# A four-layer graph network on one core: degree products of 128 columns, three products of ones ahead of one block's degrees, and row-sum copies moved ahead of the first gathered group

## The chip, the cores and the metric

The kernel runs on one core of a Trainium2 chip. The metric is the device time in microseconds (us); before the change three executions took 830.39, 831.70 and 832.74 us, median 831.7. A fourth execution was taken by the profiler; the profile and the prediction's sums are of that one. In the texts, PE is TensorE (matrix products; PEld is its weight load), ACT is ScalarE, DVE is VectorE, POOL is GpSimd and SP is the engine whose queue issues most transfers. "L964" is line 964 of the kernel before.

## The reference, cut to what matters

Four graph layers follow each other on `x` (2708 nodes, 128 features) with the same dense 2708 x 2708 matrix `adj`, each with a residual and a layer norm. The change touches the first two.

```python
# layer 0
A_hat  = A + eye;  degree = A_hat.sum(axis=1)
d      = degree ** -0.5                     # 0 where infinite
h      = (d[:, None] * A_hat * d[None, :]) @ X
x      = layernorm(x + h @ W.T + b)
# layer 1
XW     = x @ W
Z1     = leaky_relu((XW @ a_row)[:, None] + (XW @ a_col)[None, :], 0.01)
den    = exp(Z1);  num = A @ den            # num is summed over all nodes
att    = where(num != 0, den / num, 0)
x      = layernorm(x + A @ (att @ XW))
```

Layers 2 and 3 are further products with `A` (a hyperbolic layer, and one with the signs of `A`), and the kernel's change does not touch their code.

## The kernel before, in words

**Stage one, the first 120 us or so.** The transpose of `adj` is read in tiles of 512 x 512, `A{d}_{c}`: row block `d` and column block `c`, six blocks each way, the last only 148 wide. A loop over `c` (the lines up to L1280) loads the six tiles of one column block, lets ACT check them for negative values (`check`, L1236), lets DVE add them into one tile `part` (L1261, L1263), and then calls `degrees(c, part)` (L953). That folds `part` twice on DVE (L957, L958) and sums it over its 128 partitions on PE: for each of the four tiles of 128 nodes, the product of a 128 x 128 piece of `part`, as weights, with one column of ones (L964). In the traces one product of float32 operands is recorded as two matrix instructions, so a block's degrees are eight instructions. ACT then takes the square root (L975), DVE inverts it and scales the block's rows of `z = x @ W0.T`, which live in the tile `q_b` (L976 to L979), and copies the raw degrees to `row_sum` (L981).

The products with the adjacency itself are `multiply(d, c, ...)` (L940): four products of 128 x 512 into the accumulator of block `c`, with the scaled rows of block `d`. A tile above the diagonal (`d < c`) is multiplied when it is read; those on and below it are kept, and come when the degrees of their own rows are known: `row_products(c)` does row block `c` up to the diagonal. In the loop, block 1 calls `row_products(0)` ahead of its degrees, then sixteen products of bfloat16 ones (`keep_busy`, L265, into an accumulator not begun yet), and its degree products are put behind these. Blocks 2, 3 and 4 call `row_products(c - 1)` after their own degrees. `prepare_finish` (L787), called in block 2's turn, adds a few products of one or two columns (L789, L795, L800, L807).

**What sets the order.** Each engine runs its queue in the order in which it was written out. The programming framework writes it: it takes an instruction by its place in the program, but puts a later one ahead where it expects the earlier one not to be ready yet. `tc.issue_after(i)` puts the instructions of its block behind `i` on `i`'s engine, and `queued(engines)` chains all that is so marked in program order. From the trace, PE did 16 instructions of L940 between the degrees of blocks 0 and 1, then the ones, then 34 (two ahead of block 1's degrees, 32 behind) up to block 2's degrees. By their number these 34 are `multiply(0, 2)`, `multiply(1, 2)`, the whole of `row_products(1)` (16) and one product of block 3.

**Up to 225 us** the second half of layer 0 and the preparation of layer 1 follow: norms, the keys of nodes, sorting nodes into groups (24 groups of about 126, `GM`), and one-row sums over all nodes (`whole_sum`, L878), whose products fill PE between other work. These sums end in two PSUM banks, `tot[0]` and `tot[1]`: columns 0 to 2047 in four rows of the first, the rest in five pieces of the second. `sums_out` (L1479) copies pieces of them with ACT (L1482) into row 0 of `carry0`. It is called twice: for the first three pieces, columns 0 to 1535, during the sort, and for the other six at the second place described below.

**The grouped attention, from 225 us.** `adj` is split in two halves of 1354 columns. For each half and each group `q`: POOL gathers the 128 rows of the group (L1606) into one of four places; `carry` (L1637) puts the sums of `carry0` on rows 0 and 1 of the first group of a half; `numerators(q)` runs three products (L1655) into three PSUM tiles. For each of the three, DVE copies two rows to the next group's place (L1658, later L1673), and ACT takes the logarithm (L1660). Behind the third product's logarithm, ACT makes a later group's matrix (L760) from a product on PE (L757). `weighted(q - 1)` has DVE form an exponent (L1686) and ACT its exponential (L1722), and `aggregate(q - 2)` multiplies (L1750). The second `sums_out` stands in this loop at `q == 0`, behind `numerators(0)`; the second half's `carry`, at group 24, is its only reader. In the first three groups the PSUM tiles rotate over five places, so that the third product of group 2 takes the place of the first of group 1.

Of the kernel before, what the change touches and what calls it, by code (L numbers as in the profile page):

```python
# [15 lines left out]
AF = mybir.ActivationFunctionType  # L16
# [5 lines left out]
P = 128  # L22
# [3 lines left out]
NB = (N + BW - 1) // BW  # L26
# [50 lines left out]
def rows(t):  # L77
    return min(P, N - t * P)


def width(b):
    return min(BW, N - b * BW)


def tiles(b):
    return range(b * (BW // P), min(NT, (b + 1) * (BW // P)))
# [3 lines left out]
def kernel(  # L90
# [20 lines left out]
    nc = tc.nc  # L111
# [8 lines left out]
    ones = const.tile([P, P], F32, tag="ones", name="ones")  # L120
# [8 lines left out]
    one_c = const.tile([P, 1], F32, tag="one", name="one_c")  # L129
# [43 lines left out]
    row_sum = const.tile([P, NT], F32, tag="row_sum", name="row_sum")  # L173
# [40 lines left out]
    def acc_tile(b, name):  # L214
        return psum.tile([P, BW], F32, tag=f"acc{b}", name=name)

    def ps_tile(name):
        return psum.tile([P, BW], F32, tag="ps", name=name, bufs=2)
# [43 lines left out]
    def keep_busy(dst, n):  # L262

        for _ in range(n):
            last = nc.tensor.matmul(  # L265
                dst, lhsT=ones_b, rhs=ones_b.unsqueeze(1).to_broadcast([P, 4, P]), start=True, stop=True
            )
        return last.ins
# [110 lines left out]
    def c_tile(name, n=NT):  # L379
        return col.tile([P, n], F32, tag=name, name=name)  # L380
# [483 lines left out]
    sums_of = [(c, 0, BW, 32 * c, 0, 0) for c in range(4)]  # L864
# [50 lines left out]
    with tc.tile_pool(name="tri", bufs=1) as tp:  # L915
# [4 lines left out]
        acc = [acc_tile(b, f"a0_{b}") for b in range(NB)]  # L920
# [30 lines left out]
        busy = {}  # L951

        def degrees(c, part):  # L953

            w, ts = width(c), tiles(c)
            n = len(ts)
            nc.vector.tensor_add(part[:, :2, :w], part[:, :2, :w], part[:, 2:, :w])  # L957
            nc.vector.tensor_add(part[:, 0, :w], part[:, 0, :w], part[:, 1, :w])  # L958
            pd = ps_tile(f"deg{c}")
            full = [t for t in ts if rows(t) == P]  # L960
            for i, t in enumerate(ts):
                kw = rows(t)
                with tc.issue_after(busy[c]) if c in busy else nullcontext():
                    nc.tensor.matmul(  # L964
                        pd[:kw, i : i + 1], lhsT=part[:, 0, i * P : i * P + kw], rhs=ones[:, 0:1], start=True, stop=True
                    )

            span = slice(ts[0], ts[-1] + 1)
            dc = dcol[:, span]
            root = c_tile(f"droot{c}", n)  # L970
            if len(full) < n:
                nc.gpsimd.memset(root, 1.0)
            ends = [(P, 0, len(full))] + [(rows(ts[-1]), n - 1, n)] * (len(full) < n)
            for kw, ia, ib in ends:
                rooted = nc.scalar.activation(root[:kw, ia:ib], pd[:kw, ia:ib], AF.Sqrt, bias=one_c[:kw, :])  # L975
            nc.vector.scalar_tensor_tensor(dc, root, 0.0, root, op0=ALU.is_equal, op1=ALU.add)  # L976
            nc.vector.reciprocal(dc, dc)
            nc.vector.scalar_tensor_tensor(dc, root, 0.0, dc, op0=ALU.not_equal, op1=ALU.mult)
            scaled = nc.vector.tensor_mul(z[:, span, :], z[:, span, :], dc.unsqueeze(2).to_broadcast([P, n, F]))  # L979
            for kw, ia, ib in ends:  # L980
                nc.vector.tensor_copy(row_sum[:kw, ts[0] + ia : ts[0] + ib], pd[:kw, ia:ib])  # L981
            return scaled.ins, [rooted.ins]

        def unit(c):
# [238 lines left out]
        def sum_rows(n):  # L1223
            with queued(PE):
                whole_sum(n)
# [18 lines left out]
        rooted = []  # L1244
        centred(range(NB))
        for c in range(NB):
            w = width(c)
            part = ut[:, : 4 * BW].rearrange("p (t c) -> p t c", c=BW)
            at = {}
            for d in range(NB):  # L1250
                at[d] = load_tile(d, c)
                nt = len(tiles(d))
                if d < NB - 2:
                    check(d, c, at[d])
                    if (d, c) == (1, 0):
                        with tc.issue_after(checks[d, c]):
                            load_later()
                if d == 1:

                    with tc.issue_after(scaled) if scaled is not None else nullcontext():  # L1260
                        nc.vector.tensor_add(part[:, :, :w], at[0][:, :, :w], at[1][:, :, :w])  # L1261
                elif d > 1:
                    nc.vector.tensor_add(part[:, :nt, :w], part[:, :nt, :w], at[d][:, :nt, :w])  # L1263
                if d < c:
                    multiply(d, c, at[d])
                if d >= min(c, NB - 2):
                    kept[d, c] = at[d]
            if c == 1:
                product = row_products(c - 1)
                with tc.issue_after(product):  # L1270
                    busy[c] = keep_busy(acc[NB - 1], 16)
            scaled, rooted[:] = degrees(c, part)
            for d in range(NB - 2, NB):
                check(d, c, at[d])
            if c < NB - 2:
                unit(c)
            if 1 < c < NB - 1:
                row_products(c - 1)
            if c == 2:
                prepare_finish()  # L1280
# [52 lines left out]
    with ctx_keep:  # L1333
# [11 lines left out]
        with tc.tile_pool(name="sort", bufs=1) as st_p:  # L1345
# [11 lines left out]
            with queued(PE):  # L1357
                nc.tensor.matmul(
                    lim_v, lhsT=upper, rhs=filled_b[:, :, 1:], start=True, stop=False, skip_group_check=True
                )  # L1360
                for q in range(1, BQ):
                    nc.tensor.matmul(
                        lim_v[:, :, q],
                        lhsT=ones_b,
                        rhs=filled_b[:, :, before[q - 1]],
                        start=False,
                        stop=(q == BQ - 1),
# [87 lines left out]
            for i in range(2):  # L1455
                for h, (ta, tb) in enumerate(((0, t_a), (t_a, NT))):
                    low[i, h] = acc_tile(2 + 2 * i + h, f"low{i}_{ta}")
                    nn = (tb - ta) * GM
                    with queued(PE):
                        nc.tensor.matmul(  # L1460
                            low[i, h][:, :nn],
                            lhsT=upper,
                            rhs=oh[i][:, ta:tb, :],
                            start=True,
                            stop=False,
                            skip_group_check=True,
                        )
                        for t in range(tb - 1):
# [3 lines left out]
                                lhsT=ones_b,  # L1472
                                rhs=oh[i][:, t, :].unsqueeze(1).to_broadcast([P, tb - first, GM]),
                                start=False,
                                stop=(t == tb - 2),
# [3 lines left out]
            def sums_out(parts):  # L1479
                for c, a, b, o, bank, at in parts:  # L1480
                    with queued(ACT):
                        nc.scalar.copy(carry0[0:1, c * BW + a : c * BW + b], tot[bank][o : o + 1, at : at + b - a])  # L1482
# [3 lines left out]
            for i in range(2):  # L1486
# [12 lines left out]
                for t in range(NT):  # L1499
                    ohs = srt([P, P], f"ohs{i}_{t}", BF16, 10, "ohs")  # L1500
                    nc.vector.tensor_scalar(ohs, iota_b, slot[:, i, t : t + 1], None, op0=ALU.is_equal)
                    with queued(PE):
                        nc.tensor.matmul(
                            ps[:, : 6 * GM],
                            lhsT=ohs,
                            rhs=val[i][:, t, :, :].rearrange("p n g -> p (n g)"),
                            start=(t == 0),
                            stop=(t == NT - 1),
# [46 lines left out]
            with queued(ACT):  # L1555
                for g in range(FIRST):
                    group_matrix(w_first, g, gb[:, g, :])
            sum_rows(2)

    marks = {}  # L1560

# [27 lines left out]
    def grouped_attention(u_sb, rows_g):  # L1589
        adj_h = adjT.rearrange("k (h w) -> (k h) w", h=2)  # L1590
        chunks = [(0, BW), (BW, 2 * BW), (2 * BW, HALF)]
        with (
# [198 lines left out]
            for q in range(2 * GM + 2):  # L1791
                if q + 3 < 2 * GM:
                    behind = gather(q + 3)
                    if q == 3:
                        marks["begun"] = behind
                        with queued(ACT):
                            nc.scalar.dma_start(out=x_d, in_=x)
                    if q + 3 < GM:
                        group_xw(q + 3, behind)
                t = q - GM - 3  # L1800
                if 0 <= t < HALF // P:
                    with queued(PE, ACT):
                        node_major_u(t, True)
                if q == GM + GM // 4:
                    with tc.issue_after(behind):
                        fit_nodes()
                if q == GM:
                    with queued(DVE):
                        repeated(x, NF * P)
                if q == GM + 2:  # L1810
                    with queued(PE, DVE, ACT):
                        tail_factors()
                if q == GM + GM // 2:
                    with queued(DVE):
                        added_up()
                if q == GM + GM // 2 + 4:
                    with queued(PE, DVE):
                        checked()
                if q == 2 * GM - 4:
                    marks["flag"] = nc.values_load(flag_i, min_val=0, max_val=1)  # L1820
                if q < 2 * GM:
                    numerators(q)
                if q == 0:
                    sums_out(sums_of[3:])
                if 0 < q <= 2 * GM:
                    weighted(q - 1)
                if q > 1:
                    aggregate(q - 2)
# [894 lines left out]
```

## Time and profile before

| | |
|---|---|
| three executions | 830.39, 831.70, 832.74 us |
| profiled execution, its own time | 832.59 us |
| its span, first to last instruction | 830.8 us (1.8 us lie outside) |
| mean granted PE clock over the span | 0.990 |
| busy: PE, DVE, ACT, POOL | 796.2, 620.4, 518.6, 139.1 us |
| PE idle from 234.5 us on, longest piece | 0.8 us |
| degree products (L964), all blocks | 44 instructions |
| copies of the row sums (L1482) | 9, from 213.9 to 231.2 us |

A profile is one execution, taken by the hardware profiler. The table of busy time tells how much each engine worked, the chain of waits tells which piece of work was last to arrive at each point, followed back from the end, and the timeline lists the instructions of an engine in order of time with the idle time before them and who ended it. A table by stretches gives, for each stretch of the span, the busy time of each engine (with a count of instructions), the share of the full PE clock that was granted, the busy share of the DMA engines and GB/s. Times in these views count from the start of the span.

### The profile page before, as it was taken

How to read it: one execution, taken by the hardware profiler on the slowest of the kernel's cores; microseconds unless marked ns; L12 is line 12 of the kernel's file. 1: busy time of each engine (PE TensorE's matmuls, PEld its weight loads, DVE VectorE, ACT ScalarE, POOL GpSimd, SP SyncE). 2: the span in 40 equal slices, each digit the busy share in tenths (PEclk: the TensorE clock that was granted, in tenths of full speed). 3: DMA queues.
4: the chain of work that ended last, by engine and by line, in shares of the span. 5: the costliest groups of instructions: out<-in, count | busy, mean ns of one | idle time of the engine just before them, and what ended most of it. 6: DMA issues, size and time to landing. Idle time of an engine off the chain costs nothing.

```text
span 830.8 us, 10374 instructions
## 1 busy us (share of the span) xinstructions
PE 796.2 (96%) x3418; PEld 449.8 (54%) x3418; DVE 620.4 (75%) x1458; ACT 518.6 (62%) x929; POOL 139.1 (17%) x173
## 2 busy tenths in 40 slices
PE   4699999999999999999999999999999999999996
PEld 4244454454345555455554455564455666677774
DVE  3786645579689999789996677997588863776674
ACT  4955554314298998788886333696455665666662
POOL 5232000001386663162201000000000000000000
PEclk9899999999999999999999999999999999999999
DMA  9998659079589555436435778795984751856600
GB/s 341 358 384 288 142 52 358 27 262 382 174 300 391 193 164 156 142 96 213 152 101 180 269 270 296 237 336 201 358 287 156 239 190 56 291 190 243 219 36 16
DMA packets 94986, 181.71 MB, mean 219 GB/s; under 512 B 6272, under 2 KB 37396, under 8 KB 94584
## 3 DMA queue, kind: packets, MB, share of 16 engines
q1 hardware_dynamic: 85228, 142.62, 50.4%
q0 software_dynamic: 7680, 34.85, 12.9%
q10 hardware_dynamic: 2016, 3.49, 1.2%
q8 instruction: 29, 0.48, 0.2%
q14 instruction: 33, 0.27, 0.1%
HBM read 176.68 MB, written 4.28 MB: 218 GB/s over the span
## 4 chain that ended last, share of the span: by engine, by line
PE 82%; DVE 9%; DMA 5%; ACT 2%; issue 1%; SPq 1%; DVEq 0%; ACTq 0%
PE a L2052 17%; PE num L1655 13%; PE uacc L1750 11%; PE a L940 9%; PE a L2565 7%; PE a L2549 6%; PE a_u L1920 5%; DMA A<-in_adjT_dram 4%; PE a L1920 2%; PE t L878 2%; DVE jk L1413 2%; PE upper L1740 1%; PE pp L2452 1%; DVE ut L1263 1%; SPq L898 1%
## 5 line engine op out<-in xcount | busy, mean ns | idle before, releaser
L1660 ACT ACTIVATE ln<-num,inval,occ_l 128x512 f32<-128x512 f32 x144 | 99.2, 725 | 24.5 <-PE num L1655 18.2
L940 PE MATMUL a<-A,q_b 128*128 128x512 f32 (+2 forms) x264 | 109.5, 564 | 3.3 <-DVE q_b L979 3.3
L1655 PE MATMUL num<-rows_g,w_all 128*128 128x512 f32 (+1 forms) x252 | 104.5, 542 | 0.0
L1750 PE MATMUL uacc<-att,xw_g 128*128 128x512 f32 (+1 forms) x248 | 99.7, 534 | 1.4 <-issue 1.3
L2549 PE MATMUL a<-mask,node 128*128 128x452 f32 (+1 forms) x252 | 94.7, 458 | 0.0
L2052 PE MATMUL a<-cb,q_b 128*128 128x512 f32 (+1 forms) x222 | 89.5, 540 | 0.0
L1673 DVE COPY rows_g<-num 2x512 f32<-2x512 f32 x129 | 75.1, 611 | 15.6 <-ACT ln L1660 12.7
L2532 ACT ACTIVATE mask<-cb 128x904 fp32r<-128x904 f32 (+2 forms) x66 | 60.8, 922 | 34.6 <-PE a L2549 31.7
L2052 PE MATMUL a<-cb,xw 128*128 128x512 f32 (+1 forms) x196 | 79.6, 532 | 0.0
L1686 DVE SCALAR_TENSOR_TENSOR att<-q_b,e_l,ln 128x1354 f32<-128x1354 f32 (+2 forms) x50 | 77.8, 1559 | 2.1 <-ACT ln L1660 2.1
L940 PEld LDWEIGHTS a<-A,q_b 128*128 128x128 f32 (+1 forms) x264 | 46.6, 194 | 51.4 <-issue 47.3
L1606 POOL DMA_INDIRECT rows_g<-in_adjT_dram,row_i x48 | 54.1, 1127 | 116.3 <-PE num L1655 83.6
L1655 PEld LDWEIGHTS num<-rows_g,w_all 128*128 128x128 f32 x252 | 45.5, 190 | 48.9 <-issue 38.3
L2565 PE MATMUL a<-cb,edge 128*128 128x452 f32 (+1 forms) x150 | 68.9, 543 | 0.0
L1722 ACT ACTIVATE att<-att,e_l 128x1354 f32<-128x1354 f32 (+2 forms) x50 | 68.6, 1377 | 0.4 <-DVE att L1686 0.4
L1750 PEld LDWEIGHTS uacc<-att,xw_g 128*128 128x128 f32 x248 | 46.9, 190 | 38.6 <-issue 24.8
L2549 PEld LDWEIGHTS a<-mask,node 128*128 128x128 f32 x252 | 46.2, 189 | 26.6 <-issue 24.1
L1236 ACT ACTIVATE xw<-A 128x2048 f32<-128x2048 f32 (+3 forms) x36 | 57.0, 1582 | 2.7 <-DMA A<-in_adjT_dram 1.8
L2052 PEld LDWEIGHTS a<-cb,q_b 128*128 128x128 f32 x222 | 38.4, 190 | 31.6 <-issue 29.4
L1906 ACT ACTIVATE a_s<-cb 128x512 fp32r<-128x512 f32 x43 | 26.6, 626 | 40.2 <-PE a L1920 27.3
L1263 DVE TENSOR_TENSOR ut<-ut,A 128x2048 f32<-128x2048 f32 (+3 forms) x24 | 43.8, 1827 | 7.8 <-DMA A<-in_adjT_dram 7.0
L1907 DVE TENSOR_TENSOR rows_hold<-rows_hold,cb 128x452 fp32r<-128x452 f32 (+1 forms) x51 | 31.6, 626 | 18.2 <-ACT rows_hold L1906 14.7
(553 smaller groups left out, 1334.9 us busy)
## 6 DMA issues: line engine op xcount, KB each, us to landing
cb<-in_adjT_dram SPq DMA_DIRECT2D x10, 2816.0 KB
A<-in_adjT_dram SPq DMA_DIRECT2D x25, 1024.0 KB
cb<-in_adjT_dram SPq DMA_DIRECT2D x10, 2560.0 KB
B<-in_adjT_dram SPq DMA_DIRECT2D x18, 1024.0 KB
cb<-in_adjT_dram SPq DMA_DIRECT2D x5, 2486.0 KB
cb<-in_adjT_dram SPq DMA_DIRECT2D x5, 2260.0 KB
cb<-in_adjT_dram SPq DMA_DIRECT2D x2, 1554.0 KB
cb<-in_adjT_dram SPq DMA_DIRECT2D x1, 2464.0 KB
```

Source lines behind the costliest of these rows:

```text
L940: last = nc.tensor.matmul(acc[c][:, :w], lhsT=z[:kw, k, :], rhs=t[:kw, i, :w], start=c not in begun, stop=(d == NB - 1 and k == NT - 1), s ...
L1655: nc.tensor.matmul(num[:, : cb - ca], lhsT=w, rhs=gat[q][:, ca:cb], start=True, stop=True)
L1660: nc.scalar.activation(ln_n[q][:, ca:cb], num[:, : cb - ca], AF.Ln, scale=occ_l[:, g : g + 1], bias=inval[:, g : g + 1],)
L1673: nc.vector.tensor_copy(gat[q + 1][0:2, ca:cb], num[0:2, : cb - ca])
L1686: nc.vector.scalar_tensor_tensor(att[q][:, a:b], q_b[:, h * HALF + a : h * HALF + b], e2_l[:, g : g + 1], ln_n[q][:, a:b], op0=ALU.max, op ...
L1722: nc.scalar.activation(att[q][:, ca:cb], att[q][:, ca:cb], AF.Exp, bias=e1_l[:, g : g + 1])
L1750: nc.tensor.matmul(uacc[h][c][:, : cb - ca], lhsT=xw_g[:, g, :], rhs=att[q][:, ca:cb], start=(g == 0), stop=(g == GM - 1), skip_group_chec ...
L1920: nc.tensor.matmul((acc if j == 2 else upper[0])[:, :w], lhsT=parts[j], rhs=rows3[j], start=(j == 0 and not upper[1]), stop=False, skip_gr ...
L2052: nc.tensor.matmul(acc()[:, :w], lhsT=weights[:, k, :], rhs=a, start=(k == 0), stop=False, skip_group_check=True)
L2532: nc.scalar.activation(mask[:, :n, :w], hold[i][0][:, t : t + n, :w], AF.Sign)
L2549: nc.tensor.matmul(acc()[:, :w], lhsT=node[:, k, j, :], rhs=mask, start=(k == 0 and j == 0 and b != 1), stop=False, skip_group_check=True,)
L2565: nc.tensor.matmul(acc()[:, :w], lhsT=edge[:, k, :], rhs=piece(k), start=(k == 0 and b == 1), stop=False, skip_group_check=True,)
```

## The change

Three edits. The degree products take all 128 columns of the tile of ones in place of one, so that each tile of 128 nodes fills 128 columns of PSUM with equal sums; ACT and DVE read the first of each 128 columns. In block 2's turn, `row_products(1)` is written ahead of the degrees, followed by three products of bfloat16 ones, and the degree products are put behind those three. The second `sums_out` is moved out of the group loop to the end of the sort, behind the last row-sum products, and so ahead of everything of group 0 on ACT.

```diff
@@ degrees
                 with tc.issue_after(busy[c]) if c in busy else nullcontext():
                     nc.tensor.matmul(
-                        pd[:kw, i : i + 1], lhsT=part[:, 0, i * P : i * P + kw], rhs=ones[:, 0:1], start=True, stop=True
+                        pd[:kw, i * P : (i + 1) * P],
+                        lhsT=part[:, 0, i * P : i * P + kw],
+                        rhs=ones,
+                        start=True,
+                        stop=True,
                     )
 
+            sums = pd.rearrange("p (t j) -> p t j", j=P)[:, :, 0]
...
-                rooted = nc.scalar.activation(root[:kw, ia:ib], pd[:kw, ia:ib], AF.Sqrt, bias=one_c[:kw, :])
+                rooted = nc.scalar.activation(root[:kw, ia:ib], sums[:kw, ia:ib], AF.Sqrt, bias=one_c[:kw, :])
...
-                nc.vector.tensor_copy(row_sum[:kw, ts[0] + ia : ts[0] + ib], pd[:kw, ia:ib])
+                nc.vector.tensor_copy(row_sum[:kw, ts[0] + ia : ts[0] + ib], sums[:kw, ia:ib])
@@ the loop over column blocks
-            if c == 1:
+            if c in (1, 2):
                 product = row_products(c - 1)
                 with tc.issue_after(product):
-                    busy[c] = keep_busy(acc[NB - 1], 16)
+                    busy[c] = keep_busy(acc[NB - 1], (16, 3)[c - 1])
             scaled, rooted[:] = degrees(c, part)
...
-            if 1 < c < NB - 1:
+            if 2 < c < NB - 1:
                 row_products(c - 1)
@@ the end of the sort
             sum_rows(2)
+            sums_out(sums_of[3:])
@@ the group loop
-                if q == 0:
-                    sums_out(sums_of[3:])
```

## The prediction

> **What bounds the kernel now.** I read the page's chain of waits first, for the engine; then the chain in order of time around the two places that the edits touch; then the table by stretches of 1 us for the clock; last the timelines of ACT and PE around the first group.
>
> The chain by engine:
>
> ```profile
> PE 82%; DVE 9%; DMA 5%; ACT 2%; issue 1%; SPq 1%; DVEq 0%; ACTq 0%
> ```
>
> PE sets the end, so work put on PE or taken from it counts unless PE idles there. In the first stage (start, length, what):
>
> ```profile
> 59.77 0.84 DVE ut L958
> 60.74 1.02 PE deg L964 x8
> ...
> 67.13 14.70 PE a L940 x34
> 81.83 0.79 PE deg L964 x8
> 82.62 19.85 PE a L940 x46
> 102.47 0.78 PE deg L964 x8
> 103.25 15.44 PE a L940 x64
> ```
>
> Up to 60.6 the chain runs over transfers and DVE's sums; block 2's degrees hand it to PE, which keeps it to 119. So block 2's degrees are the hinge: what PE does ahead of them can hide in its wait, what comes after is paid in full. PE's own timeline shows that wait:
>
> ```profile
> 45.99 13.98 PE L940 MATMUL a<-A,q_b 128*128 128x512 f32 x32
> 60.74 1.02 PE L964 MATMUL deg<-ones,ut 128*128 128x1 f32 x8 [0.77 <-DVE ut L958]
> ```
>
> The clock in stretches (PE busy, PEld busy, DVE, ACT, POOL; then PEclk, DMA share, GB/s):
>
> ```profile
> 60.00:61.00 1.00, 0.26 (x3) 0.29 (x3) 0.60 (x1) 0.00 (x0) 1.00 (x3) 1.00 1.06 391
> 63.00:64.00 1.00, 1.00 (x3) 0.50 (x3) 1.00 (x2) 1.00 (x3) 0.00 (x0) 0.74 1.05 385
> 64.00:65.00 1.00, 1.00 (x2) 0.33 (x1) 1.00 (x1) 0.98 (x2) 0.00 (x0) 0.50 1.06 391
> 65.00:66.00 1.00, 1.00 (x3) 0.37 (x2) 0.60 (x1) 0.97 (x3) 0.00 (x0) 0.50 1.05 387
> 66.00:67.00 1.00, 1.00 (x8) 1.00 (x6) 0.15 (x1) 1.00 (x1) 0.00 (x0) 0.55 0.78 268
> ```
>
> PE is full there and gets half its clock. The missing shares are 0.26 + 0.50 + 0.50 + 0.45 = 1.71 us of PE's work, on the path.
>
> At the first group, ACT:
>
> ```profile
> 223.42 1.15 ACT L760 ACTIVATE w_first<-gb_first,bi,sc 128x126 f32<-128x126 f32 x3 [1.00 <-PE gb_first L757]
> 227.09 2.15 ACT L1660 ACTIVATE ln<-num,inval,occ_l 128x512 f32<-128x512 f32 x3 [2.52 <-issue]
> 229.14 0.45 ACT L760 ACTIVATE w_all<-gb_first,bi,sc 128x126 f32<-128x126 f32 x1
> 229.60 1.84 ACT L1482 COPY xw<-t 1x512 f32<-1x512 f32 x6
> 231.47 1.97 ACT L1660 ACTIVATE ln<-num,inval,occ_l 128x512 f32<-128x512 f32 x3
> ```
>
> ACT idles 2.52 us before group 0's logarithms and then spends 1.84 us on six copies that nobody needs for 24 groups, while PE waits twice:
>
> ```profile
> 232.30 0.32 PE L757 MATMUL num<-ident,gj_l 128*128 128x128 f32 x1 [0.45 <-issue]
> 234.49 2.51 PE L1750 MATMUL uacc<-att,xw_g 128*128 128x512 f32 x6 [1.31 <-issue]
> ```
>
> The first needs the PSUM place of group 1's first product, which its logarithm (231.47) frees; the second needs group 0's exponential, which ACT starts at 233.66. 0.45 + 1.31 = 1.76 us.
>
> **Part one: 128 columns of ones.** Eight instructions a block take 0.79 us on the chain at 81.83. No row has this very product; near are the layer's first products (128 x 128 float32, L349), twelve in 1.60 us, 0.133 each, and L1080 (128 x 130), eight in 1.09, 0.136 each. So eight take 1.07: +0.28 a block. Low end: no extra, if weight loads alone set the pace (nothing below that, since weights and count are the same). High end: L349's first 32 took 6.55 us, 0.205 each, so 1.64 and +0.85; but those were waiting on ACT's evictions, so I take +0.28. Where it lies: block 0's degrees end at about 28.3, and ACT, busy with a check until 28.7, takes the square root at 30.0, so +0.28 hides (cover gone, it would cost 0.28 of a PE that later waits anyway). Block 1's goes into the sum ahead of block 2. Blocks 2, 3, 4 are on the path: 3 x 0.28 = 0.84. Block 5 has four instructions: 0.14. That DVE and ACT read every 128th column of PSUM instead of neighbours concerns 4 values a partition in operations of 0.15 to 0.26 us; I cost it at nothing, at most 0.1 a block, and these run beside PE's next products.
>
> **Part two: three products of ones.** Sixteen run from 40.87 to 44.32: 0.216 each, 0.65 for three. The order that the edit writes, `row_products(1)` first, is what PE did already (32 instructions of L940 stand between the two degrees, which takes in its 16), so moving it costs nothing: no transfer and no queue but PE's is concerned. Behind the ones on PE stand block 2's degrees, and behind these all of block 3. Block 1's 0.28 and 0.65 make 0.93 us ahead of them, and PE's wait hides 0.77: 0.16 late. If the framework also shifts the one product of block 3 behind them, that is work moved, not added.
>
> **Part three, what these two buy: the clock.** Half clock lasts 3.41 us, 63.48 to 66.90. In the 3.41 us before it (60.07 to 63.48) PE had 0.67 idle, 1.02 of one-column products, 0.34 of two-column ones, and full products for about 1.4: 40%. A stretch around block 3's degrees (80.6 to 84.0) is three quarters full products and keeps its clock. With wide degrees and ones in the gap, about 2.2 of 3.41 us are real streaming, 65%, nearer the stretch that held. So I take the drop as gone. Both ends: 0, or 1.71 us won. Here a rule speaks against the change: the Trainium skill, "TensorE: Matmul & The Clock Gate", section "Why this matters for your kernels", asks only for no idle gap over about 3 us between matmuls. The longest gap here is 0.77 us, so by the rule nothing is to be saved, and these edits cost 0.16 + 0.84 + 0.14 = 1.14 us. The row (0.50 after a gap of 0.77) says that narrow products count little as activity, and the sum is 1.14 - 1.71 = -0.57. I follow the row.
>
> Next late: block 4's degrees at 102.31 need DVE's fold, done 101.87, 0.44 before. But DVE waited 5.17 us for tiles whose transfers wait for PE to release buffers (DMA share 0.24 from 80 to 90), so they move up with PE. I count no loss, at most 0.3.
>
> **Part four: the copies ahead of group 0.** They need the last row sums, which PE ends at 225.28; six take 1.84, so they run from about 225.3 to 227.2 in ACT's idle time. Queued behind them on ACT: group 0's logarithms, now 227.09, 0.1 later. From there ACT goes straight to group 1's logarithms at 229.7 rather than 231.47: 1.75 earlier. Their inputs are there: DVE copies group 1's rows from 228.65 and 229.51 on. Group 0's exponential moves from 233.66 to 231.9 (DVE's exponent started at 230.60 in pieces of 0.62). PE's 0.45 goes, its third product of group 2 ends at 232.7, and the accumulation starts at 232.74 instead of 234.49. Then the second exponential needs DVE's exponent of group 1, done at 235.61, and ACT would ask at 235.78: it fits by 0.17. From 234.5 on no PE idle piece exceeds 0.8 us, so the gain lasts. Ends: 0.1 lost (only the delay) to 1.76 won; I take 1.75.
>
> **Sum.** -0.57 - 1.75 = -2.32. The profiled execution took 832.59 (span 830.8 and 1.8 around it): 830.27. It lies 0.9 above the median of the runs, 831.7; from the median the sum is 829.38. I take the middle, 829.8.
>
> **Rivals.**
> 1. *The clock loss is not there in most executions, or returns elsewhere.* The same page, Part 1, has the activity window free-running, 3413 ns; this trace has 3.41 us, but no run here shows the phase shifting. If the low stretch (2.0 us) often falls across two windows, before has no loss and the widening costs its 1.14: -0.61, so 831.1. For it: runs spread over 2.35 us. Against: the low stretch fills most of a window.
> 2. *ACT's gain is swallowed*, since DVE has only 0.17 us spare at group 1: -0.57 alone, 831.1 from the median, 832.0 from the profiled one. Against: DVE idles 1.74 us just after.
> 3. *Slower: group 0's carry waits for the moved copies.* Both touch `carry0`, and now the writes come first in the program. If the framework takes the overlap by tile, DVE's L1637 starts at 227.2, not 222.17, and group 0's product, after 0.41 of copy, at 227.6, not 225.28: +2.4, ACT's gain gone, -0.57 left: +1.8, 833.5. It decides once these copies start after 224.9. Against: group 1's first product starts at about 227.6, before the copy of that place's third piece ends (228.3), so overlap is taken by columns, and these columns (up to 1353, against 1536 and more) are apart.
> 4. *Wide products at their high end*, 0.85: 0.73 ahead of block 2, 3 x 0.85 and 0.43 make 3.7, less 1.71 and 1.75: +0.2.
>
> **How the numbers follow.** Main case 0.62, 828.6 to 830.9; rival 1 0.17; rival 2 0.08; rival 3 0.08, rival 4 0.05. The range 828.6 to 832.1 leaves out rival 3 and tails of the rest. The bound of 0.3%, about what a measurement of this kernel can tell from no change, is 2.5 us: below 829.2 or above 834.2. The main case lies near the lower one: 0.38 of its 0.62 below. Slower by so much needs rival 3 or 4 without the clock's gain: 0.08. The rest, 0.54, is within.
>
> **What would show it.** Right: clock 1.00 from 60 to 67; eight degree instructions in about 1.07 us; block 2's degrees at about 60.9; block 3's about 1.3 us earlier; L1482 from 225.3, group 0's logarithms at 227.2, no idle before the accumulation at about 230 to 233. Wrong: half clock after block 2 still, degrees at 0.2 us an instruction, L1637 after 225, or a new PE wait at group 1.

## The result and the profile after

The changed kernel takes 829.72 us (median of 18 runs, 829.0 to 831.28) against 832.58 us for the kernel before (18 runs, 830.39 to 834.27): ratio 0.9971, 95% interval 0.9962 to 0.9981. That is 2.4 us, 1.6 to 3.2, inside the predicted range and 0.1 from the predicted time. The profiled execution took 829.1, its span 827.4 against 830.8.

Line numbers have moved: the degrees' product is still L964, but the square root is now L980, block sums L1266 and L1268, the copies L1487, logarithms L1666, the accumulation L1756.

The chain of waits in order of time (start, length, what), changed kernel, first stage:

```profile
60.51 0.84 DVE ut L958
...
61.49 1.13 PE deg L964 x8
...
66.20 13.84 PE a L940 x32
80.04 0.89 PE deg L964 x8
80.94 20.60 PE a L940 x48
101.54 0.89 PE deg L964 x8
102.43 15.34 PE a L940 x64
```

The hinge is still block 2's degrees behind DVE's fold, but at 61.49 rather than 60.74, and the fold itself ends later (61.35 against 60.61). Eight wide products take 0.89 us on the chain, 0.79 before: +0.10, not +0.28 (what of this is a cost comes below). Block 3's degrees are nevertheless earlier, 80.04 against 81.83, partly since they now stand one product further up. The reason is in the table by stretches (PE, PEld, DVE, ACT, POOL busy; PEclk, DMA share, GB/s):

```profile
61.00:62.00 1.00, 0.77 (x5) 0.54 (x5) 0.34 (x1) 0.00 (x0) 1.00 (x2) 1.00 1.05 391
64.00:65.00 1.00, 1.00 (x3) 0.38 (x2) 1.00 (x2) 0.98 (x4) 0.00 (x0) 1.00 1.05 387
```

The clock is 1.00 where it was 0.50. Taken alone, this profile says that the products did just what the forecast claimed. The experiments do not find the gain.

At the first group, ACT's timeline and then PE's:

```profile
223.11 1.84 ACT L1487 COPY xw<-t 1x512 f32<-1x512 f32 x6 [0.71 <-PE t L878]
224.98 2.10 ACT L1666 ACTIVATE ln<-num,inval,occ_l 128x512 f32<-128x512 f32 x3
226.97 0.46 ACT L760 ACTIVATE w_all<-gb_first,bi,sc 128x126 f32<-128x126 f32 x1
227.31 2.04 ACT L1666 ACTIVATE ln<-num,inval,occ_l 128x512 f32<-128x512 f32 x3
```

```profile
229.53 0.27 PE L757 MATMUL num<-ident,gj_l 128*128 128x128 f32 x1
230.41 2.51 PE L1756 MATMUL uacc<-att,xw_g 128*128 128x512 f32 x6
```

The copies fill what was ACT's 2.52 us of idle time, the logarithms of groups 0 and 1 follow without a gap, and neither PE row has a bracket any more: both waits (0.45 and 1.31) are gone. A measure that doesn't depend on what happened earlier is the time from group 0's first product to the first accumulation: 225.21 to 234.49 before, 9.28 us; 223.05 to 230.41 after, 7.36 us. That is 1.92 us gained.

### The profile page after: what moved, and what is told of

Same layout as the page of the kernel before. It is cut to its first block, busy times and chain, and to the rows that moved or that the text cites. A ratio compares the mean times of both kernels' runs of the same rounds, so it can differ in the third digit from the quotient of the medians.

```text
span 827.4 us, 10385 instructions
## 1 busy us (share of the span) xinstructions
PE 794.7 (96%) x3421; PEld 448.6 (54%) x3421; DVE 619.1 (75%) x1458; ACT 518.6 (63%) x929; POOL 138.0 (17%) x173
## 4 chain that ended last, share of the span: by engine, by line
PE 83%; DVE 10%; ACT 2%; issue 1%; DVEq 0%; ACTq 0%
PE a L2056 17%; PE num L1661 13%; PE uacc L1756 10%; PE a L940 10%; PE a L2569 7%; PE a L2553 6%; PE a_u L1924 5%; PE a L1924 2%; PE t L878 2%; DVE jk L1418 2%; PE pp L2456 1%; PE upper L1746 1%; DVE ut L1268 1%; PE uacc L1746 1%; PE su L302 1%
## 5 line engine op out<-in xcount | busy, mean ns | idle before, releaser
L1666 ACT ACTIVATE ln<-num,inval,occ_l 128x512 f32<-128x512 f32 x144 | 99.3, 724 | 22.6 <-PE num L1661 18.9
L1756 PE MATMUL uacc<-att,xw_g 128*128 128x512 f32 (+1 forms) x248 | 99.7, 534 | 0.1
L1612 POOL DMA_INDIRECT rows_g<-in_adjT_dram,row_i x48 | 49.3, 1028 | 114.3 <-PE num L1661 81.8
L1756 PEld LDWEIGHTS uacc<-att,xw_g 128*128 128x128 f32 x248 | 46.9, 190 | 37.3 <-issue 23.5
L1268 DVE TENSOR_TENSOR ut<-ut,A 128x2048 f32<-128x2048 f32 (+3 forms) x24 | 43.7, 1821 | 9.1 <-DMA A<-in_adjT_dram 8.3
```

What stands on the lines that cost most here:

```text
L1666: nc.scalar.activation(ln_n[q][:, ca:cb], num[:, : cb - ca], AF.Ln, scale=occ_l[:, g : g + 1], bias=inval[:, g : g + 1],)
L1756: nc.tensor.matmul(uacc[h][c][:, : cb - ca], lhsT=xw_g[:, g, :], rhs=att[q][:, ca:cb], start=(g == 0), stop=(g == GM - 1), skip_group_chec ...
```

## The experiments

Times are medians. Each ratio, with its 95% interval, is to the kernel before, run beside it on the same chip; it is not quite the quotient of the medians.

**Which part brings the gain.** Two kernels make one part alone, two leave a part of the products' edit out.

e1, the copies alone:

```diff
             sum_rows(2)
+            sums_out(sums_of[3:])
...
-                if q == 0:
-                    sums_out(sums_of[3:])
```

> The kernel before with the copies of the row sums moved and nothing else. By the traces of before and after, the moved copies bring the first accumulation 1.92 us forward (4.08 less the 2.16 that were there at group 0's first product), and 0.62 us is lost again at group 6. Theory 1 (the gain is shared): 1.3 us faster than before, 0.998 of it. Theory 2 (the copies are all of it, the PE edits are neutral): 2.4 to 2.9 us faster, 0.997. Theory 3 (the first accumulation is early, but a later wait takes it back): within 0.5 us of before.

e2, the edits to the products alone (this diff undone in the changed kernel):

> The changed kernel with the second copies of the row sums back in the group loop: wide degree products and three ones alone. Theory 1: about 1.5 us faster than before (2.86 less the 1.3 of the copies), and no half clock between 60 and 70 us. Theory 2: within 0.4 us of before. If widening costs what was predicted (1.14 us) and the clock is won only in some executions, between 0 and 0.6 us faster.

e3, the changed kernel with products of one column, and the three products of ones kept:

```diff
-                        pd[:kw, i * P : (i + 1) * P],
+                        pd[:kw, i * P : i * P + 1],
...
-                        rhs=ones,
+                        rhs=ones[:, 0:1],
```

> The changed kernel with degree products of one column again; three ones and copies as changed. If the columns keep the clock: 1 to 1.7 us slower than the changed kernel, with a half clock behind block 2's degrees. If filling the gap with ones is enough: 0.3 to 0.4 us faster than the changed kernel, since each block's eight instructions save the 0.10 us that widening cost.

e4, the changed kernel with 128 columns, without the three products of ones and with block 2's order as before:

```diff
-            if c in (1, 2):
+            if c == 1:
...
-                    busy[c] = keep_busy(acc[NB - 1], (16, 3)[c - 1])
+                    busy[c] = keep_busy(acc[NB - 1], 16)
...
-            if 2 < c < NB - 1:
+            if 1 < c < NB - 1:
```

> The changed kernel without the three products of ones and with the second block's order as before; wide degrees and copies as changed. If the ones are needed beside the columns: up to 1.7 us slower than the changed kernel, with a half clock after 63 us in the profile or a lower median clock. If the columns alone hold the clock: the same within 0.3 us, since the ones ended before the fold that the degrees wait for.

| kernel | median us | fastest to slowest | ratio and interval |
|---|---|---|---|
| before | 831.41 | 829.05 to 834.08 | |
| e1 copies alone | 829.05 | 827.85 to 833.22 | 0.9980 (0.9971 to 0.9989) |
| e2 products alone | 830.81 | 830.1 to 832.87 | 1.0000 (0.9991 to 1.0009) |
| e3 one column | 829.24 | 828.07 to 832.97 | 0.9981 (0.9970 to 0.9992) |
| e4 no ones | 829.58 | 828.66 to 831.93 | 0.9980 (0.9971 to 0.9989) |

Every kernel with the moved copies is at 0.998; the one without them is at 1.000. The gain is the copies'. In e1's trace the first accumulation is 7.36 us after group 0's first product (226.99), in e2's 9.28 (223.21), with the old wait of 1.31 us in front of it. The two rows, e1's first:

```profile
234.35 2.51 PE L1751 MATMUL uacc<-att,xw_g 128*128 128x512 f32 x6
232.49 2.51 PE L1755 MATMUL uacc<-att,xw_g 128*128 128x512 f32 x6 [1.31 <-issue]
```

The products bring nothing that can be measured: the interval of e2 admits 0.75 us either way.

e4 has a second message. Its PE timeline and its stretch from 60 to 67:

```profile
60.63 1.13 PE L964 MATMUL deg<-ones,ut 128*128 128x128 f32 x8 [0.88 <-DVE ut L958]
```

```profile
60.00:67.00 7.00, 6.37 (x28) 4.02 (x29) 5.48 (x11) 5.15 (x7) 1.26 (x2) 1.00 0.98 360
```

It waits 0.88 us there, longer than before's 0.77, and its clock stays at 1.00. In e1, with one column, the half clock is there again, from 63.40 on. The stretch of 3.41 us before it and the half clock itself, then the same two stretches of e4 (half-clock stretches of a trace begin and end on a grid of 3.41 us, its last one aside; e4's grid is counted on from the end of its first half clock, at 35.94):

```profile
59.98:63.40 3.42, 2.65 (x16) 1.72 (x14) 1.89 (x8) 1.10 (x2) 2.35 (x4) 1.00 1.05 388
63.40:66.81 3.41, 3.41 (x7) 1.55 (x6) 2.69 (x2) 3.36 (x6) 0.00 (x0) 0.50 1.03 380
59.83:63.25 3.42, 2.62 (x15) 2.02 (x16) 1.90 (x7) 1.45 (x2) 1.43 (x3) 1.00 1.05 386
63.25:66.66 3.41, 3.41 (x14) 1.89 (x13) 3.41 (x5) 3.36 (x6) 0.00 (x0) 1.00 0.98 356
```

Both first stretches hold the wait, the degrees and about 1.5 us of full products. PE is idle for as long in e4, and only e1 loses the clock. This is one trace of each, but it speaks for the forecast's view that the narrow products were what cost the clock.

**Do the copies sit on the path, and do the products of ones matter ahead of block 1?** The second set of runs, on another chip, had the changed kernel again (r1), one that makes the six copies twice (e5), one with ten instead of sixteen products of ones ahead of block 1's degrees (e6), and one with eight further products of ones right behind block 0's degrees, to keep the clock up through the first products (e7).

> The changed kernel once more, beside the others of this call on one chip, so that it can be set against the kernel with the copies alone. If the PE edits are neutral: 0.998 of before, as the copies alone were, with a smaller spread (about 2.5 us against 5). If they add to the copies: 0.9965 or less.

> The changed kernel with the six moved copies made twice in a row at their new place (the second set writes the same values). One set ends at 224.95 in the changed kernel and group 0's logarithms start at 224.98, so ACT has no time left there. If ACT sets the pace of the first groups: 1.8 us slower than the changed kernel, the first accumulation 1.8 us later. If the later wait at group 6 takes back what the copies give: 1.2 us slower. If the copies were hidden anyway: the same.

```diff
             sums_out(sums_of[3:])
+            sums_out(sums_of[3:])
```

> The changed kernel with ten products of ones ahead of block 1's degrees in place of sixteen. Theory: block 1's degrees, through the scaling of its rows, hold up DVE's sums of block 2, and so the hinge of the stage; DVE's fold for block 1 ended before PE came to it. Six ones less are 1.3 us of PE, of which up to the fold's end about 0.8 us counts: 0.5 to 0.8 us faster than the changed kernel. Rival: block 2's sums wait for transfers, so the same within 0.2 us. Or less activity brings a half clock: slower by 1 to 2 us.

```diff
-                    busy[c] = keep_busy(acc[NB - 1], (16, 3)[c - 1])
+                    busy[c] = keep_busy(acc[NB - 1], (10, 3)[c - 1])
```

> The changed kernel with eight products of ones behind block 0's degrees, where PE idles 2.6 to 3.3 us. The half clock there lasted 6.8 to 10.2 us in the profiles. Theory: with it gone by about 31 us, PE comes to block 1's degrees when DVE's fold is ready, 0.8 us earlier, and the spread of the runs shrinks: 0.5 to 0.9 us faster than the changed kernel. Rival: the ones themselves come at half clock (0.43 us each, 3.4 us) and push the first products back: the same or up to 0.5 us slower.

```diff
-                    nc.tensor.matmul(
+                    busy["last"] = nc.tensor.matmul(
...
+            if c == 0:
+                with tc.issue_after(busy["last"].ins):
+                    keep_busy(acc[NB - 1], 8)
```

| kernel | median us | ratio and interval |
|---|---|---|
| before | 832.52 | |
| r1 changed kernel | 830.79 | 0.9985 (0.9974 to 0.9997) |
| e5 copies twice | 832.16 | 1.0011 (1.0000 to 1.0022) |
| e6 ten ones | 831.98 | 1.0007 (0.9995 to 1.0019) |
| e7 warm block 0 | 832.33 | 1.0003 (0.9988 to 1.0018) |

Six more copies in ACT's queue cost 0.0026, 2.2 us (1.4 by the medians), for 1.84 us of work: ahead of group 0's logarithms ACT has room for one set (2.52 us) and not for two. e6 and e7 brought no gain. Their medians lie 1.2 and 1.5 us above r1's, and no run here shows why. In both, block 1's degrees start only when DVE's fold of block 1 is done (PE waits 1.42 and 1.54 us before them, at 44.39 and 44.34), and in r1, with all sixteen ones, they start at 44.49. So in these executions DVE's fold sets that point, and neither a faster PE nor fewer ones can move it by more than 0.15 us. In e7 the early half clock is gone, and the sixteen products ahead of the ones take 7.13 us against r1's 8.71; PE only waits the longer for it.

The four traces of this set have something that no earlier one had. DVE's timeline in r1, at group 1's rows, and PE's:

```profile
227.48 0.68 DVE L1664 COPY rows_g<-num 2x512 f32<-2x512 f32 x1 [0.18 <-PE num L1661]
230.14 0.49 DVE L1664 COPY rows_g<-num 2x330 f32<-2x330 f32 x1 [1.98 <-PE num L757]
```

```profile
230.69 0.82 PE L1661 MATMUL num<-rows_g,w_first 128*128 128x330 f32 x2 [0.75 <-DVE rows_g L1664]
232.35 2.08 PE L1756 MATMUL uacc<-att,xw_g 128*128 128x512 f32 x5 [0.84 <-issue]
```

DVE idles 1.98 us before a copy of two partitions whose input, the product, PE had finished at 228.1; PE waits for that copy and again before the accumulation. The first accumulation comes 9.17 us after group 0's first product (e5 10.57, e6 9.88, e7 9.14), so in r1's profiled execution the copies' gain is all but lost. In three of the four traces a held copy starts within 0.2 us of the end of a GpSimd gather's issue (230.14 and 229.96 in r1, 228.78 and 228.79 in e6, 229.81 and 229.63 in e7); e5's does not (230.99, the last issue ending at 229.37). In all four, GpSimd's next gather starts 0.24 us or less behind a held copy, so it can't be told which of the two engines was held first. That suggested a cause to test.

**Chip, kernel, or GpSimd?** The third set ran on a third chip: before (r2), the changed kernel (r3), the copies alone once more (r4), and the changed kernel with the gathers of keys' rows for groups 3 and 4 issued later, with group 5's (e8):

```diff
-                    if q + 3 < GM:
-                        group_xw(q + 3, behind)
+                    for g in (3, 4, 5) if q == 2 else (q + 3,) * (2 < q < GM - 3):
+                        group_xw(g, behind)
```

> The kernel before, unchanged, so that its trace and the changed kernel's come from one chip. Ratio 1.000 within 0.002. In the earlier trace of before the first accumulation came 9.28 us after group 0's first product. If the stall of some 2 us on VectorE, which all four later traces showed in the copies of group 1, comes with the chip and not with the kernels, and this chip has it, it is there in this trace as well and the figure is 10.5 to 11.5; without it, 9.28.

> The changed kernel, unchanged. Theory: the copies bring 1.9 us up to the first accumulation, of which some 0.6 is given back later, and the edits to the products bring nothing in the median, so 0.9970 to 0.9985. If the stall of VectorE isn't there, the first accumulation comes 7.36 us after group 0's first product; with it, about 9.2.

> Copies moved alone. Theory: within 0.0007 of the changed kernel's ratio on the same chip, with a wider spread of its runs (over 4 us between fastest and slowest, against 2 to 3). Rival, that the edits to the products carry part of the gain: 0.0007 to 0.0015 above the changed kernel's ratio.

> The changed kernel with the gathers of keys' rows for groups 3 and 4 issued by GpSimd later, together with those of group 5, so that none is issued while VectorE copies group 1's rows. If the gathers' issue on GpSimd holds VectorE up, the copies of group 1 show no stall and the first accumulation comes 7.36 us after group 0's first product, whatever the changed kernel itself shows on this chip. If the two have nothing to do with each other, it comes when it does in the changed kernel's own run here. Time: within 0.001 of the changed kernel's ratio, unless late rows hold a later group up, which would add 1 to 3 us.

| kernel | median us | fastest to slowest | ratio and interval | first product to first accumulation, us |
|---|---|---|---|---|
| r2 before | 832.67 | 829.17 to 835.14 | 1.0001 (0.9987 to 1.0015) | 9.27 |
| r3 changed | 829.99 | 829.21 to 831.15 | 0.9969 (0.9957 to 0.9981) | 7.37 |
| r4 copies alone | 829.16 | 828.34 to 831.82 | 0.9969 (0.9954 to 0.9984) | 7.36 |
| e8 later gathers | 829.68 | 828.99 to 831.12 | 0.9961 (0.9946 to 0.9977) | 7.36 |

No trace here has the stall, r3's neither, so e8 can't say whether the gathers cause it. It came in four of four traces of the second set and in none of the ten others. The kernel before was not profiled in that set; whether the stall belongs to that chip or to that hour, and what releases DVE, stays open. It may well be why r1's ratio is the weakest of the changed kernel's three; that is argued, not shown.

Copies alone and the whole change have the same ratio again: no gain from the products' edits shows here either. Their one visible mark is the spread. Before, e1 and r4 spread over 5.0, 5.4 and 3.5 us, and so does e3 with its one column (4.9); the changed kernel over 2.3, 1.0 and 1.9, e2 and e4 over 2.8 and 3.3 (but e5, e6 and e7 over 4.1, 3.6 and 5.4). The changed kernel loses the slowest executions and some 0.9 us of the fastest: 829.21 against r4's 828.34.

r2 is a second trace of the kernel before. Its PE timeline at block 2, and its stretch from 60 to 67:

```profile
61.17 1.02 PE L964 MATMUL deg<-ones,ut 128*128 128x1 f32 x8 [0.77 <-DVE ut L958]
```

```profile
60.00:67.00 7.00, 6.23 (x28) 3.83 (x28) 5.46 (x12) 4.72 (x7) 2.26 (x4) 1.00 0.97 354
```

This is the kernel before, unchanged, with the same wait of 0.77 us and the same narrow products, and its clock is 1.00. r4's trace, of the same products, shows the same. So the 1.71 us that the forecast saw were not in every execution: half clock there in two of the four traces without the products' edits (before and e1), and in none of the ten with one of them or both.

**What e8 showed besides.** From the first accumulation to the end of the span the kernels with the old order of copies take 596.29 (before), 596.37 (r2) and 596.38 us (e2). With the moved copies, and no stall, it is 596.97 (changed), 597.05 (e1), 597.01 (e3), 596.93 (e4), 596.79 (r3) and 597.23 (r4): 0.4 to 0.9 us of the 1.9 is given back, and PE's timelines put it at group 6's products (at 248.20 in r3). DVE comes late there because of a copy six us earlier, after which its queue runs with no wait to speak of. r3, DVE's row, and the gather that brings the rows of that copy, GpSimd:

```profile
242.17 1.69 DVE L1679 COPY rows_g<-num 2x512 f32<-2x512 f32 x3 [1.96 <-DMA rows_g<-in_adjT_dram,row_i]
```

```profile
232.49 2.83 POOL L1612 DMA_INDIRECT rows_g<-in_adjT_dram,row_i  x1 [0.30 <-issue]
```

The bracket names the transfer: DVE idles 1.96 us until rows have landed whose gather GpSimd finished issuing at 235.32, 6.85 us before. The same two in the kernel before:

```profile
243.43 1.48 DVE L1673 COPY rows_g<-num 2x512 f32<-2x512 f32 x2 [0.19 <-ACT ln L1660]
233.59 2.84 POOL L1606 DMA_INDIRECT rows_g<-in_adjT_dram,row_i  x1 [0.30 <-issue]
```

There the gather ends at 236.43, and DVE's copy starts 7.0 later without waiting for it: it was just in time. GpSimd's string of gathers starts behind group 0's weights and has no gap over 0.31 us, so the copies' move did not bring it forward. The four traces with the stall fit: their first accumulation is late, and little or nothing is given back (596.35 to 596.61). In e8, where this gather moves ahead of two others, DVE's row at the same place is

```profile
239.51 1.47 DVE L1679 COPY rows_g<-num 2x512 f32<-2x512 f32 x2 [0.19 <-ACT ln L1666]
```

The idle time is gone, and group 6's products start 16.16 us after the first accumulation (r3 16.73, before 16.15): nothing is given back there. It is lost a little later instead: PE waits 1.09 us at 252.63 for DVE's copy of a later group's rows, most likely since the postponed gathers hold that group's up (the bracket of that copy names ACT, so this is not shown). In all, e8's profiled execution needs 598.64 us from the first accumulation to the end, 1.85 more than r3's; its ratio can't be told from r3's.

## Why the prediction was right, point by point

The number was right, and the larger of its two terms was right with its mechanism. The smaller stood on one execution, and that its size came out in the profile was chance; so was the agreement of the times to 0.1 us.

**The copies: -1.75.** Right in mechanism and nearly in size. ACT's order, the logarithms of group 1 at once after group 0's, both PE waits gone: all as forecast, with -1.92 at the first accumulation (counted from group 0's first product, group 1's logarithms start 2.00 us earlier rather than 1.75, and group 0's 0.05 later rather than 0.1). Copies done twice cost 1.4 to 2.2 us, so they are on the path. The step that failed is the next one, "from 234.5 on no PE idle piece exceeds 0.8 us, so the gain lasts": it looked only at PE's idle time in the trace of before. A gather that was just in time there is 1.96 us late for DVE once everything else moves up, and 0.4 to 0.9 us go back. That leaves 1.0 to 1.5 us in the profiles. The ratios of the copies alone say 1.7 (0.9 to 2.4) and 2.6 (1.3 to 3.8); why these lie rather above the profiles isn't settled.

**The products: -0.57.** Both terms were mis-sized. The cost, put at 1.14 us, came out at 0.5. It is read from one start to the next, first in the kernel before, then in the changed one:

```profile
102.31 0.95 PE L964 MATMUL deg<-ones,ut 128*128 128x1 f32 x8
118.53 0.41 PE L964 MATMUL deg<-ones,ut 128*128 128x1 f32 x4
119.75 0.65 PE L295 MATMUL db<-ident,dcol 128*128 128x128 f32 x4 [0.22 <-DVE row_sum L981]
```

```profile
101.38 1.05 PE L964 MATMUL deg<-ones,ut 128*128 128x128 f32 x8
117.60 0.71 PE L964 MATMUL deg<-ones,ut 128*128 128x128 f32 x4
119.21 0.62 PE L295 MATMUL db<-ident,dcol 128*128 128x128 f32 x4 [0.31 <-DVE dcol L982]
```

From block 4's degrees to block 5's it is 16.22 us in both, and within 0.01 of that in all fourteen traces: block 4's wide products are 0.10 longer on the chain, and the products behind them 0.10 shorter (15.34 against 15.44). Block 3's cost nothing either: from them to block 4's it is 21.50 against 20.64, and the 0.86 is the one product that now stands behind them. Behind block 5's, where PE waits for ACT and DVE, it is 1.61 against 1.22: 0.39 for the forecast's 0.14. From block 1's degrees to block 2's it is 15.67 against 15.56: 0.11. A pair of traces whose early half clocks lie alike, r2 (27.13 to 37.37) and e2 (27.50 to 37.73), agrees: e2 is 0.37 later at block 0's degrees and 0.86 behind block 5's.

In the profiled pair shown first, the layer did end 0.57 earlier (166.59 to 166.02), to the hundredth as forecast, but with block 2's degrees 0.75 late rather than 0.16. Most of that isn't the edit's: in that execution of the changed kernel the first products ran longer at half clock (10.24 us against 6.83), and block 1's degrees were 0.64 late already. The 1.71 of clock was not there to be won in half of the traces without the edits; where it was, the edits seem to win it (e1 and e4). Half of 1.71 less 0.5 would leave some 0.35 us (an estimate from these numbers), which the interval of e2 can't tell from nothing.

**Rival 1, that the clock loss is not typical, was the right reading of this step**, and the forecast gave it 0.17. The Trainium skill, "TensorE: Matmul & The Clock Gate", Part 1, says of the activity window that it's free-running and does not restart with the kernel. The traces now show what that means: all half-clock stretches but the last are 3.41, 6.83, 10.24 or 13.65 us long, multiples of one window, and the windows fall differently in each execution. In the kernel before a window ran from 60.07 to 63.48 and took in the whole low stretch; in r2 windows end at 57.85, 61.26 and 64.67 (counted on from the end of the early half clock at 37.37), so the low stretch was shared between two, and neither, it seems, was low enough. The rule that the forecast set aside, that only gaps of over about 3 us matter, isn't rescued by this: e1 and before did lose the clock after 0.77 us.

What the forecast missed is the other half of rival 1: the loss returns elsewhere. Half clock around 169 lasts 3.41 us in before, 13.65 in r2, r4 and e1, 10.24 in r3, e3 and e4, and is absent in the changed kernel's first profile, e2's and e8's. That accounts for 1.6 of the 2.2 us by which the changed kernel was ahead at group 0 in the pair shown first (0.57 + 1.6 + 1.92, less 0.68 given back, make the 3.4 us between the two spans); and from r4 to r3, one window of 3.41 us less, PE goes from 0.3 behind at 162 to 1.3 ahead at 181, again 1.6. It can't be put down to the edits: the same kernel has it and has it not (r3 and the first profile). Whether the edits make it shorter on the average is open. For it: of the runs with one column 49 of 234 had a mean clock under 0.986 (38 of 178 of the kernel before, 7 of 34 with the copies alone, 4 of 22 of e3), of those with 128 columns 7 of 135 (none of 43 of the changed kernel itself; all 7 are e4's, e5's and e6's). Against it: the ratio of e2 doesn't move.

**The rest.** The carry did not wait for the moved copies: group 0's carry ran at 220.0, ahead of them, so rival 3, the slower one, fell. Rival 2, the gain swallowed for want of DVE's 0.17 us, fell at its place, and something like it came true one step on, through GpSimd. Rival 4 fell, the wide products being at the low end. DVE's fold for block 4 cost nothing, as counted.

So the predicted total of -2.32 stood on 1.75 of copies, which a gather cut down, and 0.57 of clock, which depends on where the window falls; the measured 2.4 us (1.6 to 3.2) is the copies' gain, as far as these runs can tell.

## What to carry to other kernels

Before a clock loss is put into a sum, see whether it lies at the same place in a second trace of the same kernel: here two of four traces did not have it. Measure an edit between two points of one trace (first product to first accumulation), so that what happened earlier in that execution drops out, and from start to start: a row that grows by 0.10 can be followed by one that shrinks by 0.10. And when one wait is taken away, follow each input of the next few steps back to its queue: a transfer issued by an engine that the edit doesn't move stays where it was, and what was just in time becomes the next wait.

## What the runs showed of the hardware

The spread of the kernel before goes with the granted clock. Over 67, 51 and 38 runs of the kernel before, the time falls by 3.3, 3.4 and 3.8 us for each 0.01 of mean clock (correlation -0.82, -0.82, -0.79). Since 0.01 of 832 us is 16.6 us at half clock, a microsecond at half clock costs some 0.2 us on the average (an estimate from these numbers), far less than the 0.5 that a stretch with PE full costs. Most of it would then fall where PE waits for others, as the early half clock does in part; this is not shown.

A GpSimd gather takes 0.95 us to issue in most rows around the first groups and 1.2 to 2.9 us in some; the longest lie beside DVE's exponents (in r3 the issues of 2.25 and 2.83 us at 229.94 and 232.49 beside exponents at 229.49 and 232.90). Over the whole traces of before, r2 and r3, 46 of the 124 issues that have a `SCALAR_TENSOR_TENSOR` of DVE running in their first 0.9 us take over 1.1 us, and 3 of the 92 others. In the four traces of the second set one issue takes 4.38 us, and DVE was held up as well, for 1.98 us at one copy in r1. No run here separates the cause.
